# The MLP's second bias moves from GpSimd to a TensorE product, and the share of other work goes from 0.70 to 0.72

## The chip, the cores and the metric

The kernel runs on one core of a Trainium2 chip. Its time is the device time of one execution in microseconds (us), and lower is better. Three executions of the kernel before took 2063.42 us in the median, 2063.11 us at the fastest and 2066.16 us at the slowest.

## The reference

The input is x with 4 batches of 1024 tokens of 256 features. Three layers follow one another, each with a layer norm (`ln`) before it:

```python
x = x + 0.5 * ffn(ln(x))       # 8 experts, the best 2 by a sigmoid router, and a shared expert
x = x + attn(ln(x))            # 16 heads of 64, and a GELU MLP inside
x = x + 0.5 * ffn(ln(x))       # the same weights again
```

The attention layer ends with the MLP whose bias `b2` is the subject here:

```python
h = att @ Wo + bo + x
y = ln(h)
m = gelu(y @ W1 + b1) @ W2 + b2
return m + h
```

## The kernel before, in words

**Numbers in two halves.** Every float32 operand of a large product is kept as two float16 numbers, a rounded one (hi) and the rest (lo). A product is three TensorE matmuls: hi·hi, hi·lo and lo·hi (`mm3`, line 970 for every matmul issued through the helper `mm`). Scales such as `CG` = 16 and `CW2` = 32 keep the halves in range. They are divided out when a result is read from PSUM.

**The main loop.** Attention runs over 4 batches x 8 pairs of heads x 2 heads x 2 halves of the queries. Each such unit has 4 steps, which makes 512 steps, one per 256 keys x 512 queries. A step `i` consists of the scores (`scores`, L1531 and L1532), an exponential on ScalarE (L570, `pt`), its rounding to float16 on ScalarE (L1543), the rest on GpSimd (L1546, both in `pk`) and the product with V (`values`, L1581 to L1584, into `av`). The row maxima for later steps (`maxima`, L1467 on TensorE and L1474 on VectorE) go 17 steps ahead. GpSimd is called POOL and ScalarE ACT, as in the profile.

**Other work.** Everything else fills the time between: the q, k, v projections of the next pair of heads (`project`), the output projection (`outproj`), the two kinds of `Job` (the expert layers `ffn` and the `mlp`), layer norms and transposes. This work is written as generators ("chains") that yield an `Ask` before each piece: an engine and an estimate of its time in us. The class `Order` is a planner which runs while the program is built. It keeps one clock for each of PE, ACT, DVE and POOL and decides in what order the pieces go into the engines' instruction streams. On the chip each engine then works its stream in that order and waits at semaphores. An estimate is thus no cost on the chip, but a change in one estimate, or in the set of pieces, may change the order of everything planned later.

**How much other work goes into a step.** `share(SHARE)` is called twice a step, once ahead of the scores and once behind them:

```python
def share(self, n):
    self.owed = max(OWED, min(self.owed + n, 1.2))
    while self.owed > 0:
        self.run(self.T["PE"])
        if not self.other(False):
            break
```

Each call adds `SHARE` us of credit, and pieces of other work go out as long as the credit is positive; each takes its estimate off. A usual piece is 1.3 us (12 matmuls of 256 columns or 6 of 512). Where the planner sees TensorE waiting (`until`), it also gives out pieces with no regard to credit, and the credit then goes negative, down to `OWED` = -16. The experts' and the MLP's jobs (rank 3) are held back by `RATE` as well: at step i they may have had at most 0.58·(i + 20) + 23.4 us of TensorE, or 0.58·(i + 40) + 23.4 where TensorE would otherwise wait. A job of nine layers goes out as a block (`block`), without a step between.

**The MLP's job.** There are 8, one for each batch and half of it (512 tokens). `prep` normalizes and transposes h, loads the saved input `x1d` into `ys`, and adds to h first `ys` (L1851) and then `b2` (L1853), both on POOL, two tiles of 256 tokens each. The tile `mb2` is `b2` copied to all 128 partitions by a DMA. `burst` is the first layer with its GELU. `second(t, hp)` is the second layer for 128 tokens: 4 x 3 matmuls of 256 columns into one PSUM bank `acc`, and `evict` adds `acc` to h on VectorE (L1892). Of the 8 jobs, 6 go into the attention loop and the 2 of the last batch come behind it, in the tail.

**The start and the tail.** Ahead of step 0 the weights are loaded, scaled and split (`setup`, with `others` for the weights of the output projection and the MLP). Step 0's scores come at about 155 us, and the last values end at about 1919 us. The tail behind them holds what the last batch still needs.

Of the kernel before, what the change touches and what calls it, by code (L numbers as in the profile page):

```python
# [7 lines left out]
F32 = mybir.dt.float32  # L8
F16 = mybir.dt.float16
I32 = mybir.dt.int32  # L10
AF = mybir.ActivationFunctionType
ALU = mybir.AluOpType
# [3 lines left out]
P = 128  # L16
D = 256
# [18 lines left out]
CG = 16.0  # L36
CW2 = 32.0
# [13 lines left out]
KW = 8  # L51
RANK, RREST = -2, -3
WAIT, AGE, LATE, LPOOL, SLOW = 2.0, 0.2, 1.6, 2.3, 0.7
SHARE, RATE, LEAD, NEAR, OWED = 0.7, 0.58, 40, 20, -16.0
BLD = 2
BU = 3
BGB = 3
# [250 lines left out]
class Kernel:  # L308
# [342 lines left out]
    def setup(self):  # L651

        nc, a, cp, ap, order = self.nc, self.a, self.cp, self.ap, self.order
        dma = nc.sync.dma_start
# [29 lines left out]
        b2 = self.tile(self.mp, [E + 1, D], F32, "fx", bufs=2)  # L684
# [128 lines left out]
        def all_qkv():  # L813
            self.stored = [0] * 3
            order.start(qkv(0), -7)
            order.start(qkv(1), -7)
            order.start(qkv(2), -7)
            yield Ask("IF", lambda: sum(self.stored) == 6)
            order.start(others(), 5)
            yield Ask("IF", lambda: all(f"bias{n}" in self.biases for n in "qkv"))  # L820
            yield Ask("DMA", 3.0)
            self.bqkv = [self.biases[f"bias{n}"] for n in "qkv"]
            self.qkv_set = order.seen

        def kept(parts, dram, at):
            t = self.tile(ap, [P, 2, S], F16, "pk", bufs=BPK)

            def to():
                for l in range(2):
                    dma(dram[l, :, at:at + S], t[:, l])  # L830

            yield from self.split(parts, t[:, 0], t[:, 1], to)
            self.setup_left -= 1

        def others():

            self.wod = self.tile(self.dp, [2, P, 8 * D], F16, "wod")
            self.mwd = self.tile(self.dp, [2, P, 2 * 2 * MH], F16, "mwd")
            wo = [self.tile(ap, [P, S], F32, "pt", bufs=BPT)[:] for i in range(2)]
            for i in range(2):  # L840
                dma(wo[i].rearrange("p (c n) -> p c n", c=4), a["Wo"][i * 4 * P:(i + 1) * 4 * P, :].rearrange("(c p) n -> p c n", p=P))
            self.bo = self.row_bcast(a["bo"], D, "bo")
            s, bc = self.cols(a["lnm_s"], 2, "lnms"), self.cols(a["lnm_b"], 2, "lnmb")
            w1, w2 = self.tile(ap, [P, S], F32, "pt", bufs=BPT)[:], self.tile(ap, [P, S], F32, "at", bufs=BAT1)[:]
            dma(w1.rearrange("p (c n) -> p c n", c=2), a["W1"].rearrange("(c p) n -> p c n", p=P))
            dma(w2.rearrange("p (c n) -> p c n", c=4), a["W2"].rearrange("(c p) n -> p c n", p=P))
            self.mb2 = self.row_bcast(a["b2"], D, "mb2")
            yield Ask("DMA", 6.0)
            jobs = [([(wo[i], None, CWO)], self.wod, i * S) for i in range(2)]
            jobs.append(([(w1[:, k * MH:(k + 1) * MH], s[:, k:k + 1], CW1) for k in range(2)], self.mwd, 0))  # L850
            jobs.append(([(w2, None, CW2)], self.mwd, S))
            for job in jobs:
                order.start(kept(*job), 5)
            yield Ask("IF", lambda: self.qkv_set)
            bv = self.tile(ap, [P, NPAIR, P], F32, "aT", bufs=BAT)
            yield Ask("DVE", 1.1)
            nc.vector.tensor_copy(bv[:], self.bqkv[2][:].unsqueeze(2).to_broadcast([P, NPAIR, P]))
            yield Ask("BANK")
            ps = self.F_()[:, :D]
            for c in range(NPAIR):  # L860
                if c % 2 == 0:
                    yield Ask("PE", 0.9)
                nc.tensor.matmul(ps, bv[:, c, :], wo[c // 4][:, c % 4 * D:c % 4 * D + D], start=(c == 0), stop=(c == NPAIR - 1))
            yield Ask("DVE", 0.42)
            nc.vector.scalar_tensor_tensor(self.bo[:], ps, 1.0 / AV, self.bo[:], ALU.mult, ALU.add)
            self.free()
            self.bo_ready = order.seen
            order.start(self.bias_cols([w1[:, :MH], w1[:, MH:]], bc, 1.0, a["b1"], "mb1"), 5)
            yield Ask("IF", lambda: "mb1" in self.biases)
            self.mb1 = self.biases["mb1"]  # L870
            self.setup_left -= 1
# [959 lines left out]
    def mlp(self, b, half, h, burst):  # L1831

        nc, mp = self.nc, self.mp
        w1, w2 = None, None
        xt, direct = None, burst

        def prep():
            nonlocal xt
            mv, r, nb = self.ln_tiles("f")
            yield from self.stats(h, mv, r, nb)  # L1840
            xt = self.half_tile()
            yield from self.transposed([h[:, t] for t in range(4)], r[:, :, 0], nb[:, :, 0], xt, not direct)
            yield Ask("LD", 2)
            ys = [self.tile(mp, [P, 2, D], F32, "ld", bufs=BLD) for g in range(2)]
            for g in range(2):
                getattr(nc, QO).dma_start(ys[g][:], self.half_of(self.x1d[b], half)[:, g * 2:g * 2 + 2])
            yield Ask("DMA", 4.5)
            for g in range(2):
                hv = h[:, g * 2:g * 2 + 2, :]
                yield Ask("POOL", 1.27)  # L1850
                nc.gpsimd.tensor_tensor(hv, hv, ys[g][:], ALU.add)  # L1851
                yield Ask("POOL", 1.27)
                nc.gpsimd.tensor_tensor(hv, hv, self.mb2[:].unsqueeze(1).to_broadcast([P, 2, D]), ALU.add)  # L1853
            self.free_ld(2)

        def burst(raw, hp):
            nonlocal w1, w2
            if direct:
                w1, w2 = self.mw
            else:  # L1860

                w = raw[:, :, 4:8].rearrange("p l c n -> p l (c n)")
                nc.sync.dma_start(w, self.mwd[:].rearrange("l p n -> p l n"))
                w1, w2 = w[:, :, :2 * MH], w[:, :, 2 * MH:]
                yield Ask("DMA", MWT)
            w1 = w1.rearrange("p l (c n) -> p l c n", c=2)
            w2 = w2.rearrange("p l (c n) -> p l c n", c=4)
            for c in range(4):
                cs = slice(c * P, (c + 1) * P)
                yield Ask("BANK")  # L1870
                yield Ask("IF", lambda: self.u_live < BU)
                self.u_live += 1
                yield Ask("PE", 1.3)
                ps = self.F_()
                for kc in range(2):
                    self.mm3(ps[:].rearrange("p (t c) -> p t c", t=4), w1[:, 0, kc, cs], w1[:, 1, kc, cs],
                             xt[:, :, kc, :], xt[:, :, 2 + kc, :], first=(kc == 0), last=(kc == 1))
                self.spawn(self.gelu_tanh(ps[:], c, hp[c], job))

        def second(t, hp):  # L1880
            yield Ask("BANK")
            yield Ask("PE", 1.3)
            acc = self.F_()[:, :D]
            ts = slice(t * P, (t + 1) * P)
            for c in range(4):
                self.mm3(acc, hp[c][:, 0, ts], hp[c][:, 1, ts], w2[:, 0, c, :], w2[:, 1, c, :],
                         first=(c == 0), last=(c == 3))

            def evict():
                yield Ask("DVE", 0.42)  # L1890
                hv = h[:, t, :]
                nc.vector.scalar_tensor_tensor(hv, acc, 1.0 / (CG * CW2), hv, ALU.mult, ALU.add)  # L1892
                self.free()
                job.evicts -= 1

            job.evicts += 1
            self.spawn(evict())

        job = Job(prep(), burst, second, 4, 5.2)
        return job  # L1900
_MAP = {"x": "L0_attn_x", "gW": "L0_ffn_gate_W", "W1f": "L0_ffn_W1", "b1f": "L0_ffn_b1", "W2f": "L0_ffn_W2",
# [26 lines left out]
```

## Time and profile before

| | |
|---|---|
| time, median of 3 runs (lowest, highest) | 2063.42 us (2063.11, 2066.16) |
| the profiled execution: its own time, its span | 2060.11 us, 2058.2 us |
| mean granted clock of TensorE | 0.994 |
| busy: PE, POOL, ACT, DVE | 1960.8, 1498.0, 1499.1, 1413.6 us |
| the additions of `b2` on POOL (L1853) | 16, 20.3 us in all, from 711.0 to 1962.4 us |

How to read it: the span is the time from the first to the last instruction, and 1.9 us of the execution's own time lie around it. Busy time is the union of an engine's instructions. PE is TensorE's matmuls, and PEld its loads of stationary operands, which go on beside them. Matmuls overlap: the time that one holds TensorE is read from the distance between the starts of neighbours and not from its duration. Line 970 stands for all matmuls that are issued through `mm`, so those are told apart by their tiles.

### The profile page before, as it was taken

What the parts mean: (1) busy time and instruction counts of PE and PEld (TensorE: products, weight loads), DVE (VectorE), ACT (ScalarE), POOL (GpSimd) and SP (SyncE); (2) the same over time, 40 slices, a digit from 0 to 9 for tenths busy, and PEclk for the clock granted to TensorE, in tenths of its full rate; (3) what the DMA queues carried; (4) which work ended last, traced back from release to release, by engine and by line L of the source; (5) the groups of instructions that cost most, each with busy time, mean ns of one, the idle gap of its engine ahead of it and who ended that gap; (6) DMA issues with size and microseconds to landing.
All of it is one profiled execution on the core that took longest, in us unless ns stands there. A gap on an engine that the chain in (4) does not pass through costs nothing. (4 is left out here: it accounts for less than half of the span.)

```text
span 2058.2 us, 53009 instructions
## 1 busy us (share of the span) xinstructions
PE 1960.8 (95%) x22468; PEld 1282.9 (62%) x22468; DVE 1413.6 (69%) x2372; ACT 1499.1 (73%) x1785; POOL 1498.0 (73%) x979
## 2 busy tenths in 40 slices
PE   6989999999999999999999999999999999999878
PEld 2546576766666556666666666656676666667545
DVE  6576676766767777775767667777767576866465
ACT  6437878768766787778787778687877777778563
POOL 7737787768767988778777887777776888778310
PEclk9999999999999999999999999999999999999999
DMA  6543233333513314243333333323324414251000
GB/s 175 152 128 84 75 91 96 75 87 61 143 36 86 89 32 108 49 100 93 81 81 70 98 76 85 92 70 76 81 48 104 114 40 106 48 111 36 11 21 21
DMA packets 213019, 166.21 MB, mean 81 GB/s; under 512 B 140991, under 2 KB 172872, under 8 KB 212782
## 3 DMA queue, kind: packets, MB, share of 16 engines
q1 hardware_dynamic: 212782, 162.83, 32.1%
q8 instruction: 176, 2.88, 0.6%
q14 instruction: 61, 0.50, 0.1%
HBM read 70.18 MB, written 13.83 MB: 41 GB/s over the span
## 5 line engine op out<-in xcount | busy, mean ns | idle before, releaser
L1546 POOL TENSOR_TENSOR pk<-pt,pk 128x1024 f16<-128x1024 f32 x512 | 1087.3, 2132 | 258.9 <-ACT pk L1543 173.0
L1474 DVE TENSOR_REDUCE mx<-S 128x1 f32<-128x1024 f32 x512 | 626.1, 1223 | 298.1 <-PE S L1467 273.1
L570 ACT ACTIVATE pt<-S 128x1024 f32<-128x1024 f32 x512 | 523.8, 1023 | 353.8 <-PE S L1532 334.5
L1543 ACT CAST pk<-pt 128x1024 f16<-128x1024 f32 x512 | 534.6, 1045 | 15.7 <-DMA aT<-pk 0.7
L1584 PE MATMUL av<-V,pk 128*128 128x65 f16 x4096 | 428.7, 192 | 25.7 <-POOL pk L1546 24.7
L1583 PE MATMUL av<-V,pk 128*128 128x64 f16 x4096 | 435.0, 195 | 0.0
L1581 PE MATMUL av<-V,pk 128*128 128x65 f16 x4096 | 434.0, 193 | 0.7 <-DVE at L1597 0.7
L1581 PEld LDWEIGHTS <-pk 128*128 128x128 f16 x4096 | 382.0, 96 | 54.0 <-issue 0.3
L1583 PEld LDWEIGHTS <-pk 128*128 128x128 f16 x4096 | 380.3, 97 | 52.9 <-issue 1.1
L1584 PEld LDWEIGHTS <-pk 128*128 128x128 f16 x4096 | 379.9, 99 | 30.9 <-POOL pk L1546 30.6
L1531 PE MATMUL S<-low 128*128 128x512 f16 x1024 | 388.2, 379 | 6.4 <-ACT pt L570 5.7
L1532 PE MATMUL S<-AC 128*128 128x512 f16 x1024 | 388.4, 379 | 0.0
L1467 PE MATMUL S<-AC 128*128 128x512 f16 x1024 | 304.4, 379 | 7.9 <-DVE mrow L1505 4.7
L970 PEld LDWEIGHTS <-hp 128*128 128x128 f16 x2100 | 204.6, 98 | 71.8 <-issue 6.2
L970 PE MATMUL F<-xA,wq 128*128 128x512 f16 x768 | 187.4, 381 | 0.0
L970 PE MATMUL F<-wfs,hp 128*128 128x256 f16 x1404 | 176.1, 273 | 1.7 <-POOL hp L1186 0.8
L1532 PEld LDWEIGHTS <-AC 128*128 128x128 f16 x1024 | 100.0, 98 | 115.1 <-issue 27.5
L1531 PEld LDWEIGHTS <-low 128*128 128x128 f16 x1024 | 100.0, 98 | 103.9 <-issue 0.6
L1186 POOL TENSOR_TENSOR hp<-u,hp 128x512 f16<-128x512 f32 x88 | 100.5, 1156 | 78.1 <-ACT hp L1183 71.5
L970 PEld LDWEIGHTS <-wfs 128*128 128x128 f16 x864 | 83.7, 99 | 111.3 <-issue 20.9
L970 PE MATMUL F<-xF,wfs 128*128 128x512 f16 x576 | 139.5, 388 | 7.6 <-DVE gb L642 4.2
L970 PEld LDWEIGHTS <-wq 128*128 128x128 f16 x768 | 74.8, 98 | 84.2 <-issue 1.9
(240 smaller groups left out, 2526.2 us busy)
## 6 DMA issues: line engine op xcount, KB each, us to landing
AC<-qk SPq DMA_DIRECT2D x128, 256.0 KB
gb<-gd SPq DMA_DIRECT2D x88, 256.0 KB
low<-qk SPq DMA_DIRECT2D x64, 256.0 KB
wq<-wqd SPq DMA_DIRECT2D x33, 384.0 KB
hp<-mwd SPq DMA_DIRECT2D x6, 1024.0 KB
x<-in_L_attn_x_dram SPq DMA_DIRECT2D x8, 512.0 KB
x1d<-x SPq DMA_DIRECT2D x8, 512.0 KB
wo<-wod SPq DMA_DIRECT2D x16, 256.0 KB
```

What stands on the lines that cost most here:

```text
L570: i = self.nc.scalar.activation(out, in_, func, **kw).ins
L970: i = self.nc.tensor.matmul(*args, start=start, **kw).ins
L1186: nc.gpsimd.tensor_tensor(hp[e][:, 1], u, hp[e][:, 0], ALU.subtract)
L1467: mm(ps[:, hs], AC[:, 0, qs], AC[:, 1, hs], start=True, stop=(h == 0 or t > 0), skip_group_check=True)
L1474: nc.vector.tensor_reduce(self.mx[:, t % 4:t % 4 + 1], ps, AX.X, ALU.max, negate=True)
L1531: mm(o, low[:, 1, ks], low[:, 0, qs], start=True, stop=False, skip_group_check=True)
L1532: mm(o, AC[:, 1, ks], AC[:, 0, qs], start=False, stop=True, skip_group_check=True)
L1543: nc.scalar.copy(pk[:, 0], pt[:])
L1546: nc.gpsimd.tensor_tensor(pk[:, 1], pt[:], pk[:, 0], ALU.subtract)
L1581: mm(o[:, 0:65], pk[:, 0, ps], v[:, 0:65], start=(n == 0 and c == 0 and t == 0), stop=False, skip_group_check=True)
L1583: mm(o[:, 0:64], pk[:, 0, ps], v[:, 65:129], start=False, stop=False, skip_group_check=True)
L1584: mm(o[:, 0:65], pk[:, 1, ps], v[:, 0:65], start=False, stop=(n == 3 and c == 1), skip_group_check=True)
```

## The change

The setup no longer copies `b2` to all partitions. It loads it as one row and makes two float16 tiles of 128 rows which are zero but for rows 0 and 64. In `mb2` these rows hold `b2`·32 as hi and lo half, and in `ones` they hold 16. In `prep` the two POOL additions of `b2` are gone. In `second` one matmul more, `ones` by `mb2`, adds `b2` to all 128 tokens of `acc`, at the scale that `evict` divides out. Its estimate for the planner goes from 1.3 to 1.41 us, and `SHARE` from 0.7 to 0.72.

```diff
-SHARE, RATE, LEAD, NEAR, OWED = 0.7, 0.58, 40, 20, -16.0
+SHARE, RATE, LEAD, NEAR, OWED = 0.72, 0.58, 40, 20, -16.0
...
-            self.mb2 = self.row_bcast(a["b2"], D, "mb2")
+            row = self.tile(self.mp, [1, D], F32, "fx", bufs=2)
+            dma(row[:], a["b2"].rearrange("(o n) -> o n", o=1))
+            self.mb2 = cp.tile([P, D], F16, tag="mb2", name="mb2")
+            self.ones = cp.tile([P, P], F16, tag="ones", name="ones")
+            yield Ask("POOL", 0.6)
+            for t in (self.mb2, self.ones):
+                nc.gpsimd.memset(t[:], 0.0)
+            for r in (0, 64):
+                nc.gpsimd.memset(self.ones[r:r + 1, :], CG)
             yield Ask("DMA", 6.0)
+            yield Ask("ACT", 0.42)
+            nc.scalar.mul(self.mb2[0:1], row[:], CW2)
+            yield Ask("DVE", 0.42)
+            nc.vector.scalar_tensor_tensor(self.mb2[64:65], row[:], CW2, self.mb2[0:1], ALU.mult, ALU.subtract)
...
                 nc.gpsimd.tensor_tensor(hv, hv, ys[g][:], ALU.add)
-                yield Ask("POOL", 1.27)
-                nc.gpsimd.tensor_tensor(hv, hv, self.mb2[:].unsqueeze(1).to_broadcast([P, 2, D]), ALU.add)
             self.free_ld(2)
...
         def second(t, hp):
             yield Ask("BANK")
-            yield Ask("PE", 1.3)
+            yield Ask("PE", 1.41)
             acc = self.F_()[:, :D]
             ts = slice(t * P, (t + 1) * P)
             for c in range(4):
                 self.mm3(acc, hp[c][:, 0, ts], hp[c][:, 1, ts], w2[:, 0, c, :], w2[:, 1, c, :],
-                         first=(c == 0), last=(c == 3))
+                         first=(c == 0), last=False)
+            self.mm(acc, self.ones[:], self.mb2[:], start=False, stop=True)
```

## The prediction

> **What bounds the kernel now.** I began with the page's busy times, then read the busy windows by stage, the waits of TensorE, the groups by shape, and last the busy windows around the POOL additions that the change removes.
>
> ```profile
> span 2058.2 us, 53009 instructions
> PE 1960.8 (95%) x22468; PEld 1282.9 (62%) x22468; DVE 1413.6 (69%) x2372; ACT 1499.1 (73%) x1785; POOL 1498.0 (73%) x979
> ```
>
> ```profile
> core 0: us, PE busy (x) PEld busy (x) DVE busy (x) ACT busy (x) POOL busy (x), PEclk, DMA share, GB/s
> 0.00:155.00 155.00, 124.24 (x771) 66.97 (x772) 100.00 (x230) 74.07 (x129) 94.05 (x120) 0.98 0.56 151
> 155.00:1913.00 1758.00, 1715.83 (x20833) 1138.46 (x20832) 1230.70 (x1957) 1351.10 (x1532) 1382.71 (x834) 1.00 0.33 80
> 1913.00:2058.00 145.00, 120.75 (x867) 77.50 (x865) 82.95 (x186) 73.93 (x124) 21.20 (x27) 0.95 0.06 19
> ```
>
> The three windows are start, attention loop and tail. TensorE bounds all three: in the loop it is busy 1715.8 of 1758 us at a granted clock of 1.00, and POOL 1382.7. Whatever is added to TensorE costs its whole time unless it falls into a wait; whatever is taken from POOL pays only where TensorE waited for POOL. How much that is stands in TensorE's waits over the whole span:
>
> ```profile
> engine line waited for: us in total, times, longest us
> PE av L1584 <- POOL pk L1546: 24.7, 25, 1.7
> PE F L939 <- ACT ld L919: 11.8, 3, 9.6
> PE S L1531 <- ACT pt L570: 5.7, 13, 1.1
> ```
>
> So 24.7 us at most can come from a faster POOL. To see when these waits come I went through TensorE's timeline step by step, from one scores product (L1531) to the next, and added up the starts' distances of matmuls that aren't attention's, and what the distances exceed the usual one for their size. Of the first 511 steps, 111 have less than 0.2 us of other work, and these lose 51.8 us of TensorE (0.47 each); the 400 others lose 24.3 us. In a step without other work TensorE has about 2.02 us to do, ACT 1.02 + 1.05 and POOL 2.13 (L570, L1543 and L1546 in the groups), so POOL leads there, and ACT is close behind. A step with one piece of 1.3 us has room for everything.
>
> **The part on POOL.** The groups by shape, then windows that begin with a pair of the additions and end with the waits behind it:
>
> ```profile
> L1546 POOL TENSOR_TENSOR pk<-pt,pk 128x1024 f16<-128x1024 f32 x512 | 1087.3, 2132 | 258.9 <-ACT pk L1543 173.0 <-issue 30.6 <-PE S L1532 20.6
> L1853 POOL TENSOR_TENSOR h<-h,mb 128x512 f32<-128x512 f32 x16 | 20.3, 1272 | 0.6
> ```
>
> ```profile
> 711.00:735.00 24.00, 21.84 (x265) 12.80 (x263) 14.13 (x19) 19.95 (x22) 23.22 (x14) 1.00 0.28 73
> 1329.00:1346.00 17.00, 14.37 (x188) 8.66 (x187) 10.02 (x15) 11.38 (x12) 16.52 (x10) 1.00 0.43 104
> 1722.00:1741.00 19.00, 17.77 (x224) 11.18 (x223) 13.25 (x17) 12.94 (x13) 18.42 (x11) 1.00 0.57 124
> 796.00:811.00 15.00, 15.00 (x193) 9.54 (x191) 11.95 (x18) 10.08 (x10) 14.74 (x9) 1.00 0.50 91
> 1206.00:1219.00 13.00, 13.00 (x165) 8.95 (x163) 9.38 (x14) 7.97 (x9) 12.89 (x8) 1.00 0.15 42
> 1626.00:1652.00 26.00, 24.81 (x306) 15.99 (x305) 17.91 (x25) 17.64 (x19) 21.44 (x17) 1.00 0.44 124
> ```
>
> Columns as above: PE is first, POOL fifth. Twelve of the 16 additions fall into the loop, as six pairs. At 711, 1329 and 1722 us POOL is full (23.22 of 24, 16.52 of 17, 18.42 of 19) and TensorE is idle 2.16, 2.63 and 1.23 us. At 796 and 1206 POOL is as full, but other work covers it and TensorE loses nothing. At 1626 TensorE loses 1.2 us, but only from 1646 on, after POOL had waited 4.3 us for a DMA (the waits of POOL: h L1307 for x1d); that isn't the additions' doing. The four in the tail stand where POOL has 21.2 us to do in 145. The gain is thus at least 0 (if ACT comes next at once), at most 12 x 1.27 = 15.2 us. I take the three windows, 2.16 + 2.54 (two additions at most) + 1.23 = 5.9 us, less the 0.8 us in them for which TensorE waited on VectorE (S L1501 for mx): **5.1 us gained**. ACT, next in line, has 4 us or more free in each.
>
> **The part on TensorE.** 32 matmuls of 256 columns come in (8 jobs x 4 tiles). The shape is in the trace: the experts' own bias product.
>
> ```profile
> 59.77 1.47 PE L970 MATMUL S<-wfs,hp 128*128 128x256 f16 x12
> 61.08 0.27 PE L970 MATMUL S<-b,gt 128*128 128x256 f16 x1
> ...
> 65.20 0.27 PE L970 MATMUL S<-b,gt 128*128 128x256 f16 x1
> 65.31 1.03 PE L970 MATMUL F<-xA,wfs 128*128 128x512 f16 x4
> ```
>
> One lasts 0.27 us, but the twelve start in 1.31 us, 0.109 each, and the next matmul starts 0.11 behind the bias product: that is its cost. Its load of `ones` (PEld, 0.098) lies beside the matmul ahead. 32 x 0.109 = **3.5 us lost**: 24 of them in the loop (2.6), 8 in the tail (0.9), which I count in full, since L970 is the largest part of the chain that ended last (4% of the span). At the lower end the tail's are hidden (2.6); at the upper each also holds its PSUM bank and `evict` (0.42) 0.11 longer, another 3.5. No wait is added: both tiles are ready over 600 us before the first use.
>
> The Trainium skill, "TensorE: Matmul & The Clock Gate", section "Back-to-back issue gap", gives sustained spacings of 81 ns at 128 and 131 ns at 512 columns; an estimate between them for 256 is 98 ns, which would make 3.1 us. The trace has 109 ns, and 215 ns at 512 (six between 76.33 and 77.62 us), so it decides. [...]
>
> **The part in the setup.** Four memsets on POOL (0.52 each at most, as L729 and L733), one scaling on ACT (0.40, as L719) and one on DVE (0.49 as L711, 2.0 as L752). They come where POOL is idle 8.2 us before 69.85, ACT 10.2 before 66.80 and DVE 6.3 before 64.05. The DMA moves 1 KB where it moved 128 KB, at 23.6 us on SP, long before it is needed. Cost 0; without that cover 4.5 us.
>
> **The part in the planner.** 0.02 x 2 x 512 = 20.5 us more credit, for the same amount of other work. Credit doesn't make work: pieces go out earlier, and the step that they leave may become empty. 20.5 / 1.3 is 16 pieces at most. Each can fill an empty step or leave one more, so the part lies between -16 x 0.47 = -7.4 us and +7.4 us. For a gain: blocks put 11.7 us of other work into one step, ten times, and the debt is then paid at 1.4 us a step, 8.4 steps, now 8.1; behind five of them I count two or three empty steps, and a third of a step off ten times is 3 steps, 1.5 us. For a loss: between jobs the work simply runs out. I take -1.0 us, nearest to the row after the blocks.
>
> **Sum.** -5.1 + 3.5 + 0 - 1.0 = -2.6 us. On the profiled execution's own time that is 2060.11 - 2.6 = 2057.5; that execution lies 3.3 us below the median of the runs, so for the median I forecast 2063.4 - 2.6 = 2060.8 us. The measurement can tell about 0.2% here, 4.1 us: this is less than that.
>
> **Rivals.**
> - Better filling. The added credit lands on empty steps: -5.1 + 3.5 - 7.4 = -9.0, or 2054.4 us. For it: 51.8 us are lost in the empty steps, more than anything else in the loop. Against: the credit's limit isn't what binds once work has run out.
> - Slower: denser filling. The pieces go out 3% faster where there is work, the two kinds of job and the projections run out sooner, and more of the 512 steps are empty. At +7.4 it makes -5.1 + 3.5 + 7.4 = +5.8, 2069.2 us; where the new order also loses the gain on POOL, 2074.3. It turns the sum into a loss from four empty steps more (1.6 us) and into one that can be told from no change from 13 (5.7 us). For it: between jobs, in steps 144 to 175 (665 to 764 us), 17 of 32 are empty already, while 284 of the 511 hold one piece (1 to 1.5 us). Against: `RATE` holds the jobs' pace as before.
> - The change relieves nothing: ACT takes POOL's place, and the 3.5 us stand, 2066.9 us. Against it: ACT has 19.95 of 24 us in the first of the windows.
>
> **How the numbers follow.** The forecast's own range, with POOL's gain from 3 to 6 and the planner within 4 us, is 2056 to 2066. It has 0.45: 0.17 faster by over 0.2%, 0.22 within, 0.06 slower. Better filling has 0.23, all faster. Denser filling 0.27: 0.26 slower, 0.01 within. Nothing relieved 0.05: 0.02 within, 0.03 slower. Together 0.40 faster, 0.25 same, 0.35 slower. Since both signs hold most of it, the range has to take in both: down to 2047 (POOL's gain at its limit of 15.2 with two thirds of the better filling, 4.9, less 3.5, is 16.6 us) and up to 2074, the densest case.
>
> **What would show it.** L1853's group gone and POOL's busy time down by about 20 us; 32 matmuls of 256 columns more, F<-mb,ones or its like, 0.109 apart. TensorE's waits on pk L1546 from 24.7 to about 20 us: right on POOL; at 24 or above: wrong. Empty steps still about 111 and their loss about 52 us: right on the planner. Step 0 still at 155 us: right on the setup. A tail that ends more than 3 us later behind the last values would be something I haven't counted. I am wrong if the number of empty steps moves by over 15.

## The result and the profile after

The changed kernel takes 2080.3 us in the median (2078.81 to 2081.51, 4 runs) against 2063.47 us before: the ratio is 1.0083 with a 95% interval of 1.0071 to 1.0095, so it is about 17 us slower. The forecast was 2060.8 us in a range up to 2074. The rival on the other side, denser filling, ended at 2069.2 and at worst at 2074.3; none of the cases held the measured time.

The profiled execution took 2080.19 us, with a span of 2078.4 us. Its page and its three stages (start, loop and tail cut at the same times as before, the tail up to the new end):

```profile
span 2078.4 us, 53055 instructions
PE 1972.4 (95%) x22500; PEld 1290.0 (62%) x22500; DVE 1416.6 (68%) x2373; ACT 1499.0 (72%) x1786; POOL 1479.8 (71%) x967
```

```profile
0.00:155.00 155.00, 119.64 (x706) 62.65 (x707) 95.10 (x215) 69.83 (x123) 88.51 (x118) 0.92 0.54 148
155.00:1913.00 1758.00, 1713.12 (x20701) 1137.19 (x20700) 1233.10 (x1965) 1338.73 (x1523) 1359.04 (x821) 1.00 0.33 80
1913.00:2078.00 165.00, 139.62 (x1098) 90.17 (x1094) 88.42 (x194) 90.47 (x141) 32.27 (x30) 0.94 0.05 17
```

What the arithmetic promised is all there: 32 matmuls more (22500 for 22468), POOL's busy time down by 18.2 us, the additions gone. But the start holds 706 matmuls where it held 771. The longest waits of TensorE (engine and line, what it waited for, us in total, times, longest), and the new product:

```profile
PE av L1596 <- POOL pk L1558: 21.2, 16, 3.1
PE F L951 <- ACT ld L931: 10.9, 3, 9.6
PE S L1543 <- ACT pt L570: 10.6, 16, 1.7
PE S L1479 <- DVE mrow L1517: 8.1, 10, 1.0
PE F L982 <- DVE gb L642: 4.7, 2, 4.2
PE F L875 <- ACT pk L620: 4.3, 1, 4.3
PE S L1479 <- DVE mx L1486: 4.1, 1, 4.1
```

```profile
L982 PE MATMUL F<-mb,ones 128*128 128x256 f16 x32 | 8.7, 273 | 0.0
```

Two waits of the kernel before that the prediction doesn't show:

```profile
PE S L1467 <- DVE mrow L1505: 4.7, 7, 0.9
PE F L863 <- ACT pk L620: 1.7, 1, 1.7
```

The wait for POOL's pk fell from 24.7 to 21.2 us. Against that stand waits that no step of the prediction had: for ACT's pt 10.6 where it was 5.7, for mrow 8.1 where it was 4.7, in the start 4.3 where it was 1.7 (pk L620) and a new one of 4.1 (mx).

To set all traces side by side I gave every matmul one price, from the distances of neighbours in the trace (0.055 us for 128 columns, 0.109 for 256, 0.215 for 512, about four times that in float32), and call the rest of the time "lost". The price for float32 is too high: in float32 neighbours stand 0.109, 0.216 and 0.43 us apart, twice as far. Some 27 us that the table calls work are therefore lost time, the same amount in both rows and in every trace below. The differences between traces, on which all that follows rests, stay as they are.

| profile | start: other work, lost | loop: lost | tail: lost | sum of work |
|---|---|---|---|---|
| before | 125.8, 25.6 | 70.8 | 29.2 | 1932.6 |
| after | 119.5, 34.9 | 76.7 | 30.7 | 1936.1 |

The difference of the spans, 20.2 us, is thus 3.5 of work, 9.3 lost in the start, 5.9 in the loop and 1.5 in the tail. The work is the prediction's 3.5. The prediction gave 0 for the start, and for the loop -1.0 from the order and -5.1 from POOL; the rest the experiments below put down to the planner's order.

A step is empty if it holds less than 0.2 us of other work. With float32 at its own distances the kernel before has the prediction's 111 empty steps, which lose 50.6 us, and the others lose 21.2; the changed kernel has 108, which lose 52.9, and the others 24.6.

### The profile page after: what moved, and what is told of

The parts are those of the page before. It is cut to its first block, busy times and chain, and to the rows that moved or that the text cites. A ratio compares the mean times of both kernels' runs of the same rounds, so it can differ in the third digit from the quotient of the medians.

```text
span 2078.4 us, 53055 instructions
## 1 busy us (share of the span) xinstructions
PE 1972.4 (95%) x22500; PEld 1290.0 (62%) x22500; DVE 1416.6 (68%) x2373; ACT 1499.0 (72%) x1786; POOL 1479.8 (71%) x967
## 4 chain that ended last, share of the span: by engine, by line
PE 84%; ACT 5%; POOL 4%; DVE 3%; issue 2%; DMA 1%; SPq 0%; POOLq 0%; ACTq 0%; DVEq 0%
PE F L982 32%; PE S L1543 10%; PE S L1479 10%; PE S L1544 10%; PE av L1596 6%; PE av L1595 6%; PE av L1593 6%; PE S L982 2%; POOL pk L1558 2%; ACT pt L570 1%; POOL hp L1198 1%; PE S L1513 1%; ACT ld L931 0%; ACT pk L1555 0%; DVE S L1183 0%
## 5 line engine op out<-in xcount | busy, mean ns | idle before, releaser
L1596 PE MATMUL av<-V,pk 128*128 128x65 f16 x4096 | 429.5, 193 | 22.2 <-POOL pk L1558 21.2
L1543 PE MATMUL S<-low 128*128 128x512 f16 x1024 | 388.7, 380 | 11.6 <-ACT pt L570 10.6
```

Source lines behind the costliest of these rows:

```text
L1543: mm(o, low[:, 1, ks], low[:, 0, qs], start=True, stop=False, skip_group_check=True)
L1596: mm(o[:, 0:65], pk[:, 1, ps], v[:, 0:65], start=False, stop=(n == 3 and c == 1), skip_group_check=True)
```

## The experiments

The kernels ran in four groups, each beside runs of the kernel before on the same chip (whose median was 2062.07, 2062.79, 2063.07 and 2063.80 us). Theory O says that the order costs the time and the arithmetic is the small sum of the prediction. Its rival A says that the arithmetic costs it. Under O, theory S puts the loss on the new setup's place in the plan, and N says that any other order than that of before is worse, whatever made it.

### Arithmetic and order apart

`plan_kept`: the new arithmetic in the old order. The planner sees the old estimates, `SHARE` is back at 0.70, and the setup's instructions go out without any estimate. The cut is against the changed kernel:

```diff
-            yield Ask("POOL", 0.6)          # and the ACT and DVE estimates of the setup
...
                 nc.gpsimd.tensor_tensor(hv, hv, ys[g][:], ALU.add)
+                yield Ask("POOL", 1.27)     # seen by the planner, no instruction
...
-            yield Ask("PE", 1.41)
+            yield Ask("PE", 1.3)
```

> The arithmetic of the change (32 products in, 16 POOL additions out, new setup) in the order that the planner made for the kernel before: the estimates that the planner sees are those of before, SHARE is 0.70, and the setup's instructions go out without estimates of their own. Theory O (the order costs the time, the arithmetic is the small sum of the prediction): 3.5 - 5.1 = -1.6 us, so 2058 to 2064 us, and a lost time ahead of step 0 of 25 to 27 us as before. Theory A (the arithmetic itself costs it, by something on TensorE or POOL that the sum lacks): 2075 us or more, as in the changed kernel.

Measured: 2058.5 us (2056.51 to 2060.3), ratio 0.9982 (0.9974 to 0.9991). In the old order the change is a gain of 3.6 us, and theory A falls. Without the new product, TensorE's sequence of matmuls is that of the kernel before but for 12 places in the tail. The waits of TensorE in it:

```profile
PE av L1593 <- POOL pk L1555: 20.2, 21, 1.7
PE F L948 <- ACT ld L928: 11.7, 3, 9.6
PE S L1540 <- ACT pt L570: 6.0, 14, 1.1
PE S L1476 <- DVE mrow L1514: 4.7, 7, 0.9
```

The wait for pk is down by 4.5 us, and those for pt and mrow stay near where they were before.

`order_of_after`: the reverse, the old arithmetic in the order of the changed kernel. The additions add the output bias, so the MLP's second bias is left out.

```diff
-            self.mm(acc, self.ones[:], self.mb2[:], start=False, stop=True)
...
                 nc.gpsimd.tensor_tensor(hv, hv, ys[g][:], ALU.add)
+                nc.gpsimd.tensor_tensor(hv, hv, self.bo[:].unsqueeze(1).to_broadcast([P, 2, D]), ALU.add)
```

> The order of the changed kernel (its estimates, SHARE 0.72) with the arithmetic of before: no product, and 16 additions of 1.27 us on POOL (of the output bias, which stands where the MLP's belongs). Theory O (order and arithmetic add up): the changed kernel's 2080 plus the 3.6 us that the arithmetic gained in the order of before, 2082 to 2086 us. If the arithmetic is what made the changed kernel slow: 2064 to 2070.

Measured: 2090.7 us, ratio 1.0132 (1.0116 to 1.0148). The sign is as O has it, but the time lies above O's range: the arithmetic is worth about 10 us in this order (1.0132 against 1.0083) and not 3.6. Its loop loses 92.8 us, and TensorE's wait for pk is 31.0 where the changed kernel has 21.2:

```profile
PE av L1596 <- POOL pk L1558: 31.0, 24, 3.0
```

### The share and the setup alone

`share72`: the kernel before with one number changed.

```diff
-SHARE, RATE, LEAD, NEAR, OWED = 0.7, 0.58, 40, 20, -16.0
+SHARE, RATE, LEAD, NEAR, OWED = 0.72, 0.58, 40, 20, -16.0
```

> The kernel before with SHARE 0.72 and nothing else. The start ahead of step 0 can't change, because credit is given from step 0 on. Theory O, with the share as a main part of it (denser filling): 2068 to 2073 us, with more empty steps or more lost in them. Theory S (the setup makes most of it, the share nearly nothing): 2060 to 2067.

Measured: 2072.09 us, ratio 1.0052 (1.004 to 1.0064). The loop loses 83.2 us, with 118 empty steps for 111. The longest single piece shows how an order can cost: in 1640 to 1660 us POOL waits

```profile
POOL h L1307 <- DMA h<-x1d: 6.1, 1, 6.1
POOL pk L1546 <- ACT pk L1543: 1.0, 1, 1.0
```

and pk is queued behind it; TensorE then loses 5.1 us in step 430, which isn't an empty step (1.3 us of other work).

`after_s70`: the changed kernel with `SHARE` back at 0.7.

> The changed kernel with SHARE back at 0.70. Theory S: 2073 to 2080, nearly all of the loss stays, with 33 to 36 us lost ahead of step 0. If the share makes the loss in the loop (5.9 us of the 20 between the profiles): 2070 to 2074. Theory A: 2078 or more.

Measured: 2093.39 us, ratio 1.0146 (1.0133 to 1.016). O and S had not expected this, and A, whose open range holds it, has fallen with `plan_kept`: the same step from 0.70 to 0.72 that costs 10 us in the kernel before gains 13 in the changed one. The share has no price of its own.

`setup_only`: the kernel before with the new setup and its estimates; the two new tiles stay unused and the additions add the output bias in place of the MLP's.

```diff
-            self.mb2 = self.row_bcast(a["b2"], D, "mb2")
+            ...                               # the new setup, as in the change
-nc.gpsimd.tensor_tensor(hv, hv, self.mb2[:].unsqueeze(1)...
+nc.gpsimd.tensor_tensor(hv, hv, self.bo[:].unsqueeze(1)...
```

> The kernel before with only the new setup (memsets, row, two halves, with their estimates); nothing uses the two tiles, the 16 POOL additions stay and add the output bias where the MLP's belongs. Theory S: the lost time ahead of step 0 goes from 25.6 to 33 to 36 us, and the time to 2070 to 2080. If the setup costs nothing, as predicted: 2061 to 2066 and 25 to 27 us lost there.

Measured: 2074.07 us, ratio 1.0059 (1.0047 to 1.0071). The start loses 32.9 us, and 6.3 us of other work that used to be done there (119.5 for 125.8) moves into the loop. The place shows in TensorE's timeline, first in the changed kernel, then in the kernel before, each with the busy windows of 90 to 100 us (columns as in the prediction's windows; TensorE's granted clock is the third number from the end):

```profile
88.21 0.38 PE L1163 MATMUL S<-gt,sel 128*128 128x512 f16 x1
92.89 2.04 PE L875 MATMUL F<-pt,aT 128*128 128x256 f32 x4 [4.31 <-ACT pk L620]
94.73 2.77 PE L982 MATMUL F<-xA,wq 128*128 128x512 f16 x6
90.00:100.00 10.00, 7.11 (x26) 3.94 (x27) 6.46 (x13) 4.03 (x8) 8.79 (x9) 0.66 0.37 131
```

```profile
86.75 0.38 PE L1151 MATMUL S<-gt,sel 128*128 128x512 f16 x1
88.85 1.97 PE L863 MATMUL F<-pt,aT 128*128 128x256 f32 x8 [1.72 <-ACT pk L620]
90.65 1.46 PE L970 MATMUL F<-xA,wq 128*128 128x512 f16 x6
90.00:100.00 10.00, 10.00 (x73) 7.14 (x72) 7.43 (x17) 5.25 (x8) 9.67 (x10) 1.00 0.32 116
```

The product of the output bias waits for ACT's rounding of the weights, which the chain `others` now starts only behind the setup's steps on ACT and DVE. (Both kernels with this setup have the wait: 4.31 us in `setup_only` too.) The waits are only half of the loss. Behind this one six matmuls of 512 columns take 2.77 us where six take 1.46, at a granted clock of 0.66 against 1.00, and the wait of 4.1 us for mx ahead of step 0 is followed by such a stretch as well: behind these two waits the changed kernel's matmuls lose 4.9 us by standing farther apart. Of the 9.3 us that its start loses beyond that of before, 4.3 are waits and 5.0 such wider spacing.

`ask_actdve`: `plan_kept` with the two steps on ACT and DVE back in the plan, ahead of the splits, without the one on POOL.

> As plan_kept (order of before), but the new setup's two steps on ACT and DVE get their estimates and their places in the chain others() ahead of the weights' splits, as in the changed kernel; the estimate on POOL stays out (with it alone the TensorE order is that of before). Theory S (these two steps hold the chain back in the plan, and the splits, the product of the output bias and the second bias come later): 8 to 14 us above plan_kept, so 2066 to 2073 us, with 33 to 36 us lost ahead of step 0 and TensorE's wait on pk L620 at 4 us instead of 1.7. Theory N (any change of the plan costs some us by chance, the start isn't special): start at 27 to 28 us lost, the time anywhere from 2055 to 2075.

Measured: 2063.38 us, ratio 1.0006 (0.9997 to 1.0015), 4.9 us above `plan_kept`, less than expected. The start loses 28.6 us where S had 33 to 36, and the wait for pk L620 that S named doesn't come; the first 64 steps lose 13.8 us for 8.7. These two steps make a part of the setup's loss. That the POOL step makes the rest together with them is inferred from the difference to `setup_only`; no run has it alone.

`own_chain`: the same setup with all its estimates, in a chain of its own behind the splits. The product and the missing additions are as in `plan_kept`.

```diff
             for job in jobs:
                 order.start(kept(*job), 5)
+            def bias_row():
+                ...                           # row, Ask("POOL"), memsets, Ask("DMA"), Ask("ACT"), Ask("DVE")
+            order.start(bias_row(), 5)
```

> As plan_kept, with the whole new setup and all its estimates in a chain of its own, started behind the four splits instead of ahead of them. The planner's order for TensorE is that of before. Theory S: as plan_kept, 2056 to 2061 us, 27 to 28 us lost ahead of step 0: the change then beats the kernel before. If the setup's instructions cost time wherever they stand: 2066 or more.

Measured: 2055.95 us (2054.52 to 2058.27), ratio 0.9968 (0.9955 to 0.998). This version beats both kernels. TensorE's order is that of `plan_kept`, and so that of before; the start loses 24.7 us. The windows of the prediction in this trace:

```profile
711.00:735.00 24.00, 23.11 (x290) 13.57 (x289) 14.29 (x19) 21.65 (x24) 22.17 (x12) 1.00 0.29 76
1329.00:1346.00 17.00, 16.52 (x200) 9.84 (x200) 11.73 (x16) 13.18 (x13) 14.43 (x8) 1.00 0.34 88
1722.00:1741.00 19.00, 18.93 (x226) 11.54 (x222) 12.76 (x16) 14.72 (x17) 15.38 (x8) 1.00 0.33 76
```

TensorE's idle time in them went from 2.16 + 2.63 + 1.23 = 6.02 us to 0.89 + 0.48 + 0.07 = 1.44: 4.6 us gained where the prediction said 5.1. This kernel is 0.9 us ahead by 711 us, so the same times hold other work. Over the same stretches of TensorE's sequence the lost time went from 3.42 + 3.67 + 1.82 us to 2.05 + 1.20 + 0.64, in `own_chain` and `plan_kept` alike: 5.0 us gained.

### Why the loop is worse in another order

`quiet_s70`: the changed kernel at share 0.7 with the setup out of the plan, so that only the estimates of the product and of the additions differ.

> The changed kernel with SHARE 0.70 and the new setup without estimates, so that only the estimates of the product (1.41 for 1.3) and of the missing additions differ from the order of before. The start and the first batch are then as in plan_kept: 27 to 28 us lost ahead of step 0. Theory S: 2056 to 2064 us, near plan_kept's 2058.5. Theory N: the order differs from the first MLP job on (about step 160), and the loop's loss may move by 5 to 15 us either way; 2065 us or more speaks for N.

Measured: 2080.22 us, ratio 1.0083 (1.0068 to 1.0099). The start loses 27.7 us, as in `plan_kept`, and the loop 87.0 for 64.3. Theory S alone isn't enough. The next four start from `own_chain`:

```diff
-                yield Ask("POOL", 1.27)       # est_pool: the estimate without an instruction goes
...
-            yield Ask("PE", 1.3)              # est_pe
+            yield Ask("PE", 1.41)
...
-SHARE, RATE, ... = 0.7, 0.58, ...             # own_s72, own_s69
+SHARE, RATE, ... = 0.72 (0.69), 0.58, ...
```

> own_chain, but the planner no longer sees the 1.27 us of the missing POOL additions; the product's estimate stays 1.30, SHARE 0.70. The order is that of before up to the first MLP job. Theory P (the missing POOL estimate alone makes the loss of quiet_s70, since it frees POOL in the plan): 2075 to 2082 us, and TensorE's waits for mrow at 12 us. Theory N (the order of before is a lucky one, and any other one is worse by some amount that nothing in the edit tells): anywhere from 2058 to 2085, with no relation to quiet_s70.

> own_chain with the product's estimate at 1.41 instead of 1.30, the POOL estimate of the additions still in the plan, SHARE 0.70. Theory P: 2054 to 2060 us, like own_chain, since the estimate only becomes truer. Theory N: worse by 5 us or more, 2061 or above, although each estimate is nearer to the chip's.

> own_chain with SHARE 0.72. If the share's 10 us of share72 are its own (pieces go out earlier, steps run empty): 2064 to 2069 us. If they come from where single orders happen to put a piece: anywhere from 2050 to 2075; the number of empty steps then stays within 5 of own_chain's 94 while the time moves.

> own_chain with SHARE 0.69, the other direction. If the share acts steadily (denser filling costs, looser gains): 2048 to 2055 us. Theory N: above own_chain's 2056 too, since another order is drawn; 2058 to 2075.

Measured: `est_pool` 2077.05 (ratio 1.007, 1.0055 to 1.0085), `est_pe` 2079.71 (1.0084, 1.0069 to 1.0099), `own_s72` 2070.72 (1.0036, 1.0023 to 1.0049), `own_s69` 2071.75 (1.0043, 1.0028 to 1.0058). By the ratios all four are worse than `own_chain` by 14 to 24 us, the share in both directions, and each of the two estimates although it is the truer one. That agrees with theory N, and P is out with `est_pe`.

To see whether an estimate acts by what it says, the last four change as little as still moves the order:

```diff
-            yield Ask("PE", 1.3)              # tiny_pe
+            yield Ask("PE", 1.31)
...
-SHARE, ... = 0.7, ...                         # own_s701
+SHARE, ... = 0.701, ...
...
+                if b < 2:                     # est_late
                     yield Ask("POOL", 1.27)
...
-                yield Ask("DVE", 0.42)        # tiny_dve, the MLP's evict
+                yield Ask("DVE", 0.44)
```

> own_chain with the product's estimate at 1.31 instead of 1.30, 0.01 us: too little to mean anything on the chip, enough to make another order from about step 200 on (8308 rows of TensorE's listing move). Theory N (the order of before is a lucky draw, any redraw of this length costs): 2066 to 2080 us. Theory T (what costs is that the estimates of est_pe and est_pool tell the planner something it handles badly): 2054 to 2060, like own_chain.

> own_chain with SHARE 0.701, which moves 908 rows, some hundred us of the loop. Theory N: between own_chain's 2056 and 2066 us, in proportion to the short stretch that is redrawn. If SHARE itself acted, a twentieth of 0.72's 15 us: 2057.

> As est_pool, but the POOL estimates are missing only for the last two batches, so the order is that of before up to about step 410. Theory N: the loss comes only behind the first difference, 0 to 7 us, 2056 to 2063, and nothing lost ahead of it beyond own_chain's. If the missing estimates act through the jobs of the early batches on everything: the same.

> own_chain with the estimate of the MLP's evict at 0.44 instead of 0.42 us; 564 rows move, from about step 460 on. Theory N: 2055 to 2062 us. A control: no more than the stretch behind the first difference can change.

Measured: `tiny_pe` 2082.56 us (ratio 1.0092, 1.0077 to 1.0107), `own_s701` 2056.68 (0.9967, 0.9955 to 0.9979), `est_late` 2064.14 (1.0004, 0.9995 to 1.0014; 1 us beyond what was expected), `tiny_dve` 2061.1 (0.9988, 0.9978 to 0.9997). By the ratios, an estimate that moves by 0.01 us costs about 26 us (1.0092 against 0.9968). In the loop's first 192 steps, ahead of the first difference, `tiny_pe` loses 28.9 us where `own_chain` loses 28.7; behind it 58.9 against 34.6. A longer redraw costs more. Counted in the traces, as places of TensorE's sequence that hold another matmul than in `own_chain`, 740 and 1197 places (`tiny_dve`, `own_s701`) cost 0 to 4 us, 2082 (`est_late`) 7, and 6922 to 11535 (`own_s72`, `own_s69`, `tiny_pe`, `est_pe`, `est_pool`) 14 to 26.

TensorE's waits in the loop, `own_chain` and then `tiny_pe`:

```profile
PE av L1601 <- POOL pk L1563: 20.4, 21, 1.7
PE S L1548 <- ACT pt L570: 6.3, 15, 1.1
PE S L1484 <- DVE mrow L1522: 4.7, 7, 0.9
```

```profile
PE av L1601 <- POOL pk L1563: 26.4, 22, 2.6
PE S L1548 <- ACT pt L570: 11.9, 21, 1.1
PE S L1484 <- DVE mrow L1522: 8.0, 10, 0.9
```

The loss is spread over three waits of attention's own chain (15 of the 24 us) and isn't a single event. The one on mrow can be counted: after a unit's transposed maxima TensorE waits for VectorE, 0.7 to 0.8 us in the mean. That happened 7 times in 128 units in the kernel before and in `own_chain`, 10 in the changed one, `share72` and `tiny_pe`, 14 in `after_s70` and 15 to 17 in `quiet_s70`, `est_pe`, `est_pool` and `own_s69`.

The number of empty steps, 108 to 123 in all of these, doesn't tell the time: the changed kernel has the fewest. What they lose moves more. Of the 24 us that `tiny_pe`'s loop loses beyond `own_chain`'s, 16.8 lie in empty steps (65.4 for 48.6), though there are only 114 for 111. An empty step has no fixed price: in the kernel before, the first of a run of empty steps loses 0.28 us, the second 0.50, the third 0.91 and those behind it 0.51 (51, 25, 15 and 20 of them).

Open stays why the order of before is better than every other order that was redrawn at length (nine of them, with 77 to 91 us lost in the loop against 63 to 71 in the old one). That its constants were chosen for it would explain that, but no run shows it.

## Why the prediction was wrong

**POOL, right.** 5.1 us were expected, from three windows; the same stretches of work give 5.0 in `own_chain` and `plan_kept`, and TensorE's wait for pk fell by 4.5 in `plan_kept`. In another order the same removal is worth about 13.6 us, 10.1 by `order_of_after` and the product's 3.5, still within the bound of 15.2. The arithmetic as a whole, -5.1 + 3.5 = -1.6 in the prediction, came out as -3.6 in `plan_kept` and -6.6 by the ratio of `own_chain`. The pairs that the windows called covered gave next to nothing: in `plan_kept` the 64 steps around the one at 1206 us lose 4.4 us for 4.3, those around the one at 1626 us 6.8 for 7.3.

**TensorE, right.** The product costs 0.109 us each: twelve starts of the second layer from 780.71 to 782.01 us, then the product. 3.5 us of work are in the sum of every trace with the product. `plan_kept` gained 3.6 us by loading an engine busy 95% to relieve one busy 73%, since the first waited for the second. The sustained spacings of the Trainium skill ("TensorE: Matmul & The Clock Gate", "Back-to-back issue gap"), from which I estimated 98 ns for 256 columns, aren't what this trace has: 109 ns.

**The setup, wrong.** I looked for cover on the chip, found it (POOL idle 8.2 us, ACT 10.2) and wrote 0. The instructions as such cost nothing that shows: in `own_chain`, which has them all, the start loses 24.7 us for 25.6. What I missed is that an `Ask` in the chain `others` holds back everything that the chain starts later, in the plan. The four splits slipped, with them the output bias, and 9.3 us went in the start (`setup_only`: 7.3), 4.3 in waits and 5.0 in matmuls that stand farther apart, nearly all of it behind the two new waits of over 4 us, at a lower granted clock. The prediction had no term for either. The 4.5 us without cover were no upper end either: they priced the instructions and not the chain behind them.

**The planner, wrong, and the largest error.** I priced the share by its sense, 20.5 us of credit over empty steps, between -7.4 and +7.4, and took -1.0. It has no such sense. The step that failed is to treat the rest of the order as kept, and to look only at the number that was edited. A new estimate redraws everything behind it, and a long redraw cost 14 to 26 us against `own_chain`. That should have been its own term: the 1.41 for 1.30 alone (`est_pe`) is worth 24 us, and I gave it none. Nor is an empty step worth a flat 0.47 us. (The debt's 8.4 and 8.1 steps differ by 0.23 and not by a third, so my -1.5 was -1.1 by its own terms; it changes nothing.) My sign for this part was not the right one either: 108 empty steps and 52.9 us lost in them read as "right on the planner", while the time moved by 17 us.

**The rivals.** Denser filling had the right sign for the wrong reason: empty steps fell from 111 to 108, and only 2.3 of the 5.9 us that the loop lost more lie in them. The case that relieves nothing is refuted by `plan_kept`.

## What to carry to other kernels

Where a planner lays out the instructions while the program is built, a change has two effects, its arithmetic and the redraw of the order. They can be measured apart: keep the old estimates for the planner and change only the instructions. If the old order is better than its neighbours, as it was here, the redraw is a cost of its own, of any edit to an estimate, and its size has to come from how other orders do and not from what the edit means. New work in a setup belongs in a chain of its own, behind what others wait for.

## What the runs showed that I had not expected

An estimate of 1.31 for 1.30 us costs about 26 us with the same matmuls on TensorE. Moving 15 us of POOL work in the loop to TensorE is worth 4 us or 10, depending on the order around it. And the granted clock in the start fell as well: 0.92 in the first 155 us of the changed kernel, 0.98 before. A part of that is in the stretches behind long gaps of TensorE (0.66 from 90 to 100 us, after the wait of 4.3 us); in the first 50 us, ahead of any difference in the order, the two kernels had 0.93 and 0.97, and `plan_kept` and `own_chain`, in one order, had these two values as well.
